# Gated layers of a four-layer trunk: each depthwise convolution in four pieces of four rounds in place of eight pieces of two

## The chip, the cores and the metric

The kernel runs on one core of a Trainium2 chip. The metric is the device time of one execution in microseconds. TensorE (PE in the profile) multiplies, its weight loads are shown apart as PEld; VectorE is DVE, ScalarE is ACT, GpSimd is POOL, and SyncE (SP) issues most of the DMA.

## What is computed

The input x has 512 channels of 64x64 pixels in float32. Four layers follow each other, each as x + f(groupnorm(x)): layer 0 is attention with eight heads, layers 1 and 2 are gated convolutions, layer 3 is a linear attention. The change touches layers 1 and 2, whose f is this (cut to the core; `conv1x1` is a matrix product over channels with a bias):

```python
fused = conv1x1(x, w_in, b_in)              # 512 -> 1024 channels
pwa = fused[:, :128]
abc = fused[:, 128:]                        # 896 channels, 7 groups of 128
dw0, dw1, dw2 = split(dwconv7(abc, dw_w, dw_b), (128, 256, 512))
h = pwa * dw0
h = conv1x1(h, pw0_w, pw0_b) * dw1
h = conv1x1(h, pw1_w, pw1_b) * dw2
x = x + conv1x1(h, w_out, b_out)
```

`dwconv7` is a depthwise 7x7 convolution: every channel with its own 49 taps.

## The kernel before

x stays in SBUF as X, four groups of 128 channels by 4096 pixels. `_attention` does layer 0, `_gated_convs` (lines 1110 to 1388) layers 1 and 2 in one loop over the layers, `_linear_attention` layer 3.

The depthwise convolution runs on TensorE. Each group of 128 channels is written to DRAM as planes (`_PlaneConv.put` and `take`, lines 938 to 977, tile `plane`, DRAM tensor `F`): the pixels of a channel are split by row modulo 4 and column modulo 8 into 32 planes. A convolution then is a product with small matrices T that carry taps from 32 planes to 32 planes. For one group `_PlaneConv.conv` (line 1014) works in `FORM.nr` = 16 rounds. A round is 24 products: 3 row offsets, 2 halves `rho`, 4 column groups `g`, each with a 64x32 tile of weights and 128 columns; each product is two weight loads and two matmuls in the trace, so a round has 48 matmul records. Four rounds fill a pair of PSUM banks (`ps_cv`, four banks, so two pairs), which VectorE transposes to the result `h` (line 1060); after the last round it transposes four quarters of `h` (line 1066), and ScalarE adds a bias to each (line 1317).

What a round reads is loaded by `load` (line 979) for two rounds at a time (NL = 2): SyncE issues one DMA for T and two for S, and ScalarE copies each 32 partitions of S, shifted, to 32 others (line 1006). Four buffers of each are there. `ahead` loads the first four rounds before a convolution begins; within it, round r loads what round r+4 needs.

`conv` is a generator. Between its pieces `convolve` (line 1311) puts other work in the program: parts of the input products of later groups (`group`, seven steps of a product scheme with seven instead of eight multiplications, lines 1230 to 1260), the products of the gates (`gate`, line 1262) and of the output (`output`, line 1277). They are 128x128 tiles by 512 columns, each two weight loads and two matmuls in the trace, into four banks `ps`, and leave by VectorE and by ScalarE's `kept` copies (line 1209). Where a piece ends is set here:

```python
for r0 in range(0, f.nr, f.rounds):
    ps = [self.psum.tile([P, BLK], FP, tag="mm", name="ps_cv") for _ in range(2)]
    for r in range(r0, r0 + f.rounds):
        if r % f.run == 0 and r > r0:
            yield
        if r % self.nl == 0:
            if r + f.rounds < f.nr:
                self.ready.append(self.load(i, hf, wT, r + f.rounds))
            w, S = self.ready.pop(0)
...
    if r0 + f.rounds < f.nr:
        yield
```

`f.rounds` is 4, and `f.run` is 2: a piece has two rounds, and each convolution eight pieces. `convolve` shares out the work in between: it has a list with a weight for each item, computes `parts = FORM.nr // FORM.run` (line 1324), and after each piece hands out items up to an equal share; the last quarter of the list is kept for the four quarters at the end.

TensorE's order is that of the program: `_PlaneConv.matmul` (line 933) pins each product to it, which is why all of them bear line 933 in the profile. The other engines' order is made by the layer that records the program[...].

Layer 3 uses `_PlaneConv` too, with `FORM3`, whose rounds have 16 products and whose pieces have four rounds; the change doesn't touch it.

## Time and profile before

| | us |
|---|---|
| median of three runs | 3827.91 |
| lowest, highest | 3826.85, 3833.11 |
| span of the profiled execution | 3828.3 |
| first and last convolution matmul of layers 1 and 2 | 2330.7, 3133.7 |

In the stretch from 2320 to 3130 us:

| engine, operation | count | mean ns |
|---|---|---|
| PE matmul of a convolution, 64x32 tile, 128 columns | 10656 | 272 |
| PE matmul of w_out, 128x128 tile, 512 columns | 347 | 602 |
| ACT copy within S | 224 | 1269 |
| DVE transpose of ps_cv to h | 110 | 1048 |
| DVE transpose within h | 52 | 1227 |

A matmul's mean is from its start to its modelled end; matmuls overlap, so the distance from one start to the next is shorter than that, and a row of the timeline that merges many of them is read by the start of the row after it. The page divides the span into 40 slices of 95.7 us. "Issue" is time in which an engine waited for nothing that the profile shows.

### The profile page before, as it was taken

How to read it: one execution, taken by the hardware profiler on the slowest of the kernel's cores; microseconds unless marked ns; L12 is line 12 of the kernel's file. 1: busy time of each engine (PE TensorE's matmuls, PEld its weight loads, DVE VectorE, ACT ScalarE, POOL GpSimd, SP SyncE). 2: the span in 40 equal slices, each digit the busy share in tenths (PEclk: the TensorE clock that was granted, in tenths of full speed). 3: DMA queues.
4: the chain of work that ended last, by engine and by line, in shares of the span. 5: the costliest groups of instructions: out<-in, count | busy, mean ns of one | idle time of the engine just before them, and what ended most of it. 6: DMA issues, size and time to landing. Idle time of an engine off the chain costs nothing. (4 is left out here: it accounts for less than half of the span.)

```text
span 3828.3 us, 81625 instructions
## 1 busy us (share of the span) xinstructions
PE 3752.0 (98%) x35294; PEld 1657.9 (43%) x35294; DVE 2688.1 (70%) x3242; ACT 2069.3 (54%) x2998; POOL 132.2 (3%) x112
## 2 busy tenths in 40 slices
PE   6999999999999999999999999999999999999999
PEld 5633334333365333343333334554445544455543
DVE  6577787777765777876776757766677677665437
ACT  3577774777735777746665655663246632355210
POOL 0000000000000000000000000000000000122112
PEclk9999999999999999999999999999999999999999
DMA  2000000000000000000000015772057730564312
GB/s 100 9 1 1 1 1 9 1 1 1 1 1 9 1 1 1 1 9 1 1 1 1 1 49 168 198 201 81 13 157 194 199 102 27 151 178 103 97 56 91
DMA packets 178413, 212.91 MB, mean 56 GB/s; under 512 B 13032, under 2 KB 121832, under 8 KB 177920
## 3 DMA queue, kind: packets, MB, share of 16 engines
q1 hardware_dynamic: 151232, 148.46, 14.5%
q10 hardware_dynamic: 26784, 59.11, 4.2%
q8 instruction: 280, 4.59, 0.5%
q14 instruction: 85, 0.70, 0.1%
q0 software_dynamic: 32, 0.06, 0.0%
HBM read 147.81 MB, written 59.77 MB: 54 GB/s over the span
## 5 line engine op out<-in xcount | busy, mean ns | idle before, releaser
L753 ACT ACTIVATE pt<-ps_s,A 128x512 f32<-128x512 f32 x2048 | 1286.3, 687 | 534.8 <-PE ps_s L745 527.1
L832 DVE TENSOR_TENSOR acc<-acc,pt 128x1024 f32<-128x1024 f32 x960 | 1174.1, 1223 | 327.8 <-ACT pt L753 300.8
L745 PE MATMUL ps_s<-O,K 64*64 64x512 f32 x8192 | 1111.6, 589 | 0.0
L745 PEld LDWEIGHTS ps_s<-O,K 64*64 64x64 f32 x8192 | 334.3, 133 | 553.8 <-issue 307.1
L765 PE MATMUL av<-pt,O 64*64 64x512 f32 x4096 | 558.2, 590 | 0.9 <-ACT pt L753 0.9
L765 PE MATMUL av<-pt,V 64*64 64x512 f32 x4096 | 554.4, 590 | 0.0
L1006 ACT COPY S<-S 32x1295 f32<-32x1295 f32 (+1 forms) x272 | 341.4, 1256 | 217.4 <-DMA S<-F 105.6
L765 PEld LDWEIGHTS av<-pt,O 64*64 64x64 f32 x4096 | 171.5, 133 | 276.1 <-issue 254.9
L765 PEld LDWEIGHTS av<-pt,V 64*64 64x64 f32 x4096 | 168.3, 133 | 281.0 <-issue 270.3
L933 PE MATMUL ps<-diff,w_sum 128*128 128x512 f32 x516 | 242.0, 601 | 3.1 <-DVE w_sum L441 1.9
L933 PEld LDWEIGHTS ps_cv<-S,T 64*32 64x32 f32 x13824 | 194.1, 105 | 111.5 <-issue 73.0
L933 PE MATMUL ps_cv<-S,T 64*32 64x128 f32 x13824 | 233.6, 273 | 5.0 <-issue 2.4
L933 PE MATMUL ps<-h,w_out_L 128*128 128x512 f32 x512 | 229.6, 599 | 1.5 <-DVE X L1287 1.4
L454 DVE TENSOR_TENSOR diff<-X 128x512 f32<-128x512 f32 x200 | 134.0, 683 | 83.1 <-PE ps L933 46.4
L383 ACT ACTIVATE X<-X,gn_less 128x512 f32<-128x512 f32 x122 | 77.3, 709 | 152.0 <-DVE gn_less L125 152.0
L933 PE MATMUL ps<-X,w_in_L 128*128 128x512 f32 x304 | 145.8, 611 | 10.8 <-ACT w_in_L L391 5.4
L933 PE MATMUL ps<-h,pw_L 128*128 128x512 f32 x320 | 143.8, 599 | 1.9 <-DVE h L1275 1.6
L933 PEld LDWEIGHTS ps<-h,w_out_L 128*128 128x128 f32 x512 | 94.0, 190 | 118.3 <-issue 96.5
L933 PEld LDWEIGHTS ps<-diff,w_sum 128*128 128x128 f32 x516 | 94.6, 190 | 116.8 <-issue 106.5
L454 DVE TENSOR_TENSOR diff<-X,diff 128x512 f32<-128x512 f32 x200 | 135.3, 683 | 12.9 <-PE ps L933 11.3
L1060 DVE STREAM_TRANSPOSE h<-ps_cv 128x512 f32<-128x512 f32 x112 | 109.2, 1048 | 48.6 <-PE ps_cv L933 48.2
L933 PE MATMUL ps<-agg,w_proj 128*128 128x512 f32 x256 | 118.5, 602 | 1.0 <-DVE turned L1060 0.9
(233 smaller groups left out, 3324.7 us busy)
## 6 DMA issues: line engine op xcount, KB each, us to landing
T<-in_L_T_dram SPq DMA_DIRECT2D x112, 384.0 KB, 4.6
F<-plane ACTq DMA_DIRECT2D x112, 324.0 KB, 3.5
S<-F SPq DMA_DIRECT2D x224, 162.0 KB, 4.6
S<-G SPq DMA_DIRECT2D x96, 153.0 KB, 4.3
G<-plane ACTq DMA_DIRECT2D x48, 289.0 KB, 2.5
row<-G SPq DMA_DIRECT2D x48, 272.0 KB, 3.3
T<-in_L_T_dram SPq DMA_DIRECT2D x48, 256.0 KB, 4.1
out_dram<-y SPq DMA_DIRECT2D x32, 256.0 KB, 2.0
```

Of the source, the lines that this page charges most:

```text
L383: self.nc.scalar.activation(xs, xs, AF.Identity, bias=less)
L454: yield eng.tensor_tensor(t[j][c], a(c), b(c), ALU.subtract)
L745: nc.tensor.matmul(ps[ts(half, D), ts(h, BLK)], K[rows, t * P + half * D : t * P + (half + 1) * D], QO[pair][rows, cols], start=True, stop ...
L753: exp = nc.scalar.activation(pt[:, ts(h, BLK)], ps[:, ts(h, BLK)], AF.Exp, bias=A[:, t, h : h + 1])
L765: nc.tensor.matmul(av[half][rows, :], v[keys, t * P + h * D : t * P + (h + 1) * D], pt[keys, ts(h, BLK)], start=(t == 0), stop=(t == NT - 1),)
L832: add = nc.vector.tensor_add(acc, acc if u > 1 else first, pt)
L933: self.tc.keep_in_program_order(self.nc.tensor.matmul(*args, **kw))
L1006: nc.scalar.copy(second, first)
L1060: nc.vector.transpose(out, src)
```

## The change

One number of the form of layers 1 and 2 changes, `run` from 2 to 4:

```diff
-FORM = _Form(2, 1, 4, 8, 1, 2, 3, 1, (-1, -1, -1, -1), (0, 0, 0, 0, -1, -1, -1, -1))
+FORM = _Form(4, 1, 4, 8, 1, 2, 3, 1, (-1, -1, -1, -1), (0, 0, 0, 0, -1, -1, -1, -1))
```

The inner `yield` of `conv` is then never reached, so that a piece is the four rounds of one pair of banks, 192 matmul records, and a convolution has four pieces. `parts` in `convolve` becomes 4, so the same items are handed out in stretches of about twice the length. The number of products, loads, copies and transposes stays as it is. The loads of rounds r+4 and r+6 are issued in the program with no other work in between. `run` is used nowhere else; the data in DRAM, the buffers and the banks are as before.

## The prediction

> **What bounds the kernel now.** I read the page first: engines and slices, the groups of TensorE instructions by shape, the instruction queues under DMA. Then the timeline of TensorE inside the two gated layers, which the change alone touches (2331 to 3134 us of the span), and the waits there.

> ```profile
> span 3828.3 us, 81625 instructions
> PE 3752.0 (98%) x35294; PEld 1657.9 (43%) x35294; DVE 2688.1 (70%) x3242; ACT 2069.3 (54%) x2998; POOL 132.2 (3%) x112
> PEclk9999999999999999999999999999999999999999
> ...
> q8 instruction: 280, 4.59, 0.5%
> ```

> TensorE sets the end: 98% busy at full clock, VectorE and ScalarE have room. What shortens TensorE's own sequence shortens the kernel, and what makes it stand still lengthens it. The q8 line (transfers, MB, share of the DMA engines) is used below.

> ```profile
> 3050.28 1.59 PE L933 MATMUL ps_cv<-S,T 64*32 64x128 f32 x96
> 3051.80 2.84 PE L933 MATMUL ps<-h,w_out_L 128*128 128x512 f32 x6
> 3054.57 1.60 PE L933 MATMUL ps_cv<-S,T 64*32 64x128 f32 x96
> 3056.10 2.84 PE L933 MATMUL ps<-h,w_out_L 128*128 128x512 f32 x6
> ...
> 3411.03 2.20 PE L933 MATMUL ps_cv<-S,T 64*32 64x128 f32 x128
> 3413.16 5.42 PE L933 MATMUL ps<-agg,w_proj 128*128 128x512 f32 x12
> ```

> Pieces of convolution alternate with stretches of dense products; the next row's start says what a row really takes. A piece of two rounds is 96 matmul records; start to start it takes 1.525 us (1.53, 1.52 here). Dense stretches of 4, 6, 8, 10 and 12 records take 1.914, 2.773, 3.631, 4.489 and 5.348 us: 0.429 each and 0.198 once per stretch. Pieces of 128 records in the last layer take 1.961 to 1.978 at best, so a conv record costs (1.97-1.525)/32 = 0.0140, and 1.525-96x0.0141 = 0.17 us is paid once per piece.

> ```profile
> 2413.85 1.98 PE L933 MATMUL ps<-X,w_in_L 128*128 128x512 f32 x4
> 2415.77 1.54 PE L933 MATMUL ps_cv<-S,T 64*32 64x128 f32 x90
> 2417.66 0.42 PE L933 MATMUL ps_cv<-S,T 64*32 64x128 f32 x6 [0.35 <-issue]
> ```

> From the waits of the same stretch, 2320 to 3130 us:

> ```profile
> PEld ps_cv L933 <- issue: 55.1, 75, 1.0
> PEld ps_cv L933 <- ACT S L1006: 19.7, 26, 0.8
> ```

> Here a piece stops after 90 of its 96 matmuls, with nothing in the profile to wait for ("issue"). Six pieces of the 112 do this, with 0.25 to 0.88 us lost, 3.5 us in all. Counting TensorE's instructions (weight load and matmul each one), the six resume at 40299, 41323, 42603, 42859, 43627 and 55402: whole multiples of 256 apart, to one instruction. Queue q8 has 280 transfers of 16 KB for TensorE's some 71,200 instructions, one per 256, and the transfer in question began 2.45 to 2.77 us before each resume. These stops are instruction fetch.

> [...] 0.17 + 0.198 us per pair of changes between 64x32 and 128x128 tiles. [...] 192 instructions in 1.36 us (0.0071 each) beat the fetch.

> **The change, part by part.** The order of TensorE's instructions in the built program shows 56 pieces of 192 records in place of 112 of 96; matmuls are the same, and 12 semaphore waits are added among some 24,000 instructions (nothing).

> (1) Fewer changes of tile shape. 112-56 = 56 pairs go, each 0.17+0.198 = 0.366 us: -20.5 us, all on TensorE, so all on the path.

> (2) Instruction fetch. In the kernel before, a block of 256 instructions can never lie in one piece (192), so it always takes in a dense stretch of at least 8 instructions: the shortest blocks take 1.525+1.914+0.4 = 3.8 us (the trace's least are 3.73 to 3.84). The fetch of a block is asked for about when its predecessor is entered. From that entry to the transfer's start the trace has two clusters, 0.6 to 1.0 and 1.5 to 2.3 us, earlier or below zero where a dense stretch let the sequencer run ahead (by up to some 40 instructions); from the transfer's start to use 2.2 to 2.8. Sum 3.2 to 4.3 us against 3.8: it nearly always just fits, and six times doesn't. That fit is the cover, and the change removes it: a piece now has 384 instructions, and a block wholly inside takes 256x0.0071 = 1.81 us. The stop is then 3.2-1.81 = 1.4 to 4.3-1.81 = 2.5 us.
> How many: laying the 256-grid of the six stops over the changed order, 29 of 95 blocks in these layers lie wholly in one piece (the kernel before: none); by proportion it would be (384-256)/404 = 32%, 30 blocks. 15 of them begin 57 or more instructions into the piece, past the sequencer's lead: 15 x 1.95 = 29 us. 14 begin within the first 43, where the lead may have called the fetch during the dense stretch: between 0 and 2.2, I take 1.1: 15 us. Some four more take in a last dense instruction or two, 0.5 each: 2. Sum +46 us, bounds 27 (15x1.4 + 14x0.4) and 76 (29x2.5 + 4). The 3.5 us of today's six stops go.

> (3) ScalarE, SyncE, DMA. Loads (one T, two S each) stay eight per convolution; two now come at the head of a piece together, and a few w_out loads of SyncE move by one or two loads. Buffers (four) come free one piece earlier or later, so from free to use there are two double stretches and a piece (2x3.6+3.04 = 10.3 us) where there were four single stretches and three pieces (12.2). Landing takes 4.6 us (S) and two copies 2x1.27, 7.1: 3 us spare. The four S copies of a piece stand closer, so a `kept` copy (0.69) can stand behind one or two more; its waits on TensorE today are 10.3 us at weight loads, most of it hidden. I take 0, bounds 0 and +6; gain excluded, nothing here gets shorter.

> (4) VectorE, PSUM. Same eight transposes (1.05) and four (1.23) per convolution, in pairs after each piece. Longest burst: six w_out products in 5.3 us against two transposes and six 0.73 additions, 6.4; the first product ends at 0.9, its bank is free at 2.9, the fifth wants it at 3.4 (four banks). No stop: 0. Conversely five data waits behind today's pieces (at 2397, 2515, 2885, 2924 and 3002 us; 0.84 to 1.51 each, 5.3 in all) may vanish under fetch stops, as other engines catch up: 0 to -5, I take 0.

> Sum: 3828.3 - 20.5 - 3.5 + 46 = 3850.3. The profiled span (3828.3) and the median of the runs shown (3827.9) agree to 0.4, so 3850 us.

> **The rivals.** (A) is the forecast: slower, 3850; own range 3832 to 3880 by its bounds.
> (B) Faster: the fetch keeps up. Mechanism: the sequencer's lead over the array. If it asks for each block long before the predecessor is entered, blocks arrive in time, only (1) stays: 3828.3-20.5-3.5 = 3804. For it: transfers have begun 1 to 7 us before that entry where dense stretches stood ahead (they get longer now), and 14 of 29 blocks begin near one. Against: inside pieces transfers begin 0.6 us after entry at the earliest, and the six stops exist. It decides where the mean stop of the 29 falls under 24/29 = 0.83 us, i.e. entry to use under 2.64 us; the trace has 3.2 there at best.
> (C) Slower through data: the second pair of rounds in a piece, with no dense stretch ahead of it any more, waits for its S copy. With the longest such wait of today (0.8) in each of 56 pieces: +45-20.5-3.5 = 3849 without (A), about 3895 on top of it. For it: ScalarE stands 105.6 us waiting for S transfers in these layers. Against: the 3 us to spare in (3).
> (D) The change doing nothing it says is excluded by the built order (56 pieces); that (1) and (2) cancel within 0.2% (under 7.7 us) is the low end of (A): stops of 0.6 to 1.1 us a block.

> **How the numbers follow.** A 0.65, B 0.15, D 0.08, C (with A or alone) 0.12. A change of 0.2%, 7.7 us, is about what a measurement of this kernel can tell from no change. Faster is B, 0.15; same is D, 0.08; slower is A and C, 0.77. Range: up to A's upper bound, 3880, leaving some 0.07 of C out; down to 3812, between B and D, leaving most of B out (0.13).

> **What would show it.** Pieces of 192 records: undisturbed 2.88 us start to start; about half should be interrupted inside by one "issue" gap of 1 to 2.5 us, all on the 256-grid, some 2.5 us after a q8 transfer began. Issue gaps at conv weight loads grow by some 40 us; TensorE's busy share falls. Dense stretches keep 0.429 per record. If pieces run 2.88 us throughout, (2) is wrong and B holds; if gaps end with an S copy rather than "issue", C. The size of a stop, not the count, is the least sure term.

## The result and the profile after

The changed kernel takes 3861.36 us (median of 5 runs, 3860.07 to 3866.26); the kernel before, with its runs beside these, 3830.03 (5 runs, 3826.85 to 3833.50). The ratio is 1.0082, 95% interval 1.0071 to 1.0093: slower by 31 us where 22 were forecast. The profiled spans are 3859.8 and 3828.3, 31.5 apart.

From the page of the changed kernel:

```profile
span 3859.8 us, 81643 instructions
PE 3745.8 (97%) x35294; PEld 1667.7 (43%) x35294; DVE 2689.0 (70%) x3242; ACT 2066.5 (54%) x2998; POOL 131.6 (3%) x112
PEclk9999999999999999999999999999999999999999
...
q8 instruction: 280, 4.59, 0.5%
```

TensorE has as many instructions and less busy time (3745.8 for 3752.0), in a longer span: it stands still more. The timeline of TensorE in the gated layers shows where (columns: start, time taken, then the instructions; idle time ahead of them in brackets):

```profile
2908.63 0.65 PE L933 MATMUL ps_cv<-S,T 64*32 64x128 f32 x25 [2.37 <-issue]
...
2912.83 2.96 PE L933 MATMUL ps_cv<-S,T 64*32 64x128 f32 x192
2915.73 1.98 PE L933 MATMUL ps<-diff,w_sum 128*128 128x512 f32 x4
...
2510.57 2.63 PE L933 MATMUL ps_cv<-S,T 64*32 64x128 f32 x169
2515.82 0.64 PE L933 MATMUL ps_cv<-S,T 64*32 64x128 f32 x23 [2.62 <-issue]
2516.39 1.98 PE L933 MATMUL ps<-diff,w_sum 128*128 128x512 f32 x4
```

An undisturbed piece of 192 records runs from 2912.83 to 2915.73, 2.90 us (the least in the stretch is 2.84). The piece at 2510.57 stops after 169 records, waits 2.62 us for nothing that the profile shows, and ends at 2516.39. From the waits of the same stretch, 2320 to 3141 us (who waited for whom: us in all, times, longest):

```profile
PEld ps_cv L933 <- issue: 71.8, 68, 2.9
PE ps_cv L933 <- issue: 35.6, 28, 2.6
PEld ps L933 <- ACT kept L1209: 18.2, 10, 5.6
PE ps L933 <- ACT kept L1209: 10.4, 8, 4.8
PEld ps_cv L933 <- ACT S L1006: 6.1, 8, 0.8
```

The second, third and fourth of these rows in the kernel before:

```profile
PE ps_cv L933 <- issue: 2.2, 5, 0.7
PEld ps L933 <- ACT kept L1209: 10.3, 12, 1.7
PE ps L933 <- ACT kept L1209: 5.4, 7, 1.4
```

What grows most is the idle time without a cause in the profile, and more ahead of the convolution's matmuls (2.2 to 35.6 us) than of their weight loads (55.1 to 71.8).

From the starts of TensorE's records I took, for each, what the distance to the next exceeds the usual one by, and sorted the excess between the first and the last convolution matmul of layers 1 and 2. A stop is put down to the fetch if it ends where a block of 256 instructions begins, on the grid that the kernel before gave; dense matmuls at twice their usual distance are counted apart.

| excess, us (cases) | before | after | difference |
|---|---|---|---|
| stops where a block of 256 begins | 3.7 (8) | 44.3 (33) | +40.6 |
| dense matmuls at half rate, 0.853 in place of 0.429 | 2.0 (5) | 7.8 (18) | +5.8 |
| all other waits of TensorE | 15.9 | 19.9 | +3.9 |
| changes of tile shape saved, 56 x 0.366 | | | -20.5 |

The sum is +29.8 against 31.5 between the spans; 1.7 us stay unexplained. The last row isn't measured: it is the price of the prediction.

That the stops on the grid are stops of the fetch has two signs. In both kernels every stop of over 0.2 us between two matmuls of a piece lies on the grid, 6 of 6 before and 30 of 30 after, and none elsewhere. And those of the changed kernel end 2.2 to 2.9 us after a transfer of q8, the queue that carries the instructions, began; that queue made 280 transfers of 16 KB for some 71,200 instructions of TensorE, one to some 256.

The half rate follows some of the long stops, and a long data wait too. Windows of the changed kernel (from and to in us, length, busy time and records of TensorE, granted clock, DMA share, GB/s), around a stop of 2.18 us in the piece from 2420 and after a data wait at 2927:

```profile
2418.00:2424.00 6.00, 4.96 (x194) 1.00 0.45 145
2426.00:2429.00 3.00, 3.00 (x5) 0.52 1.03 276
...
2921.00:2926.00 5.00, 5.00 (x198) 1.00 0.77 245
2931.00:2937.00 6.00, 4.56 (x6) 0.52 0.02 4
```

The granted clock is 1.00 before and 0.52 after: five or six dense matmuls take twice their time. By the clock record of the trace half the clock is granted for 23.9 us of these layers (3.4 in the kernel before): 10.2 after three of the stops, which end at 2412.03, 2424.94 and 2624.13 us, 6.8 after the data wait, and 6.8 at the change from layer 1 to layer 2, where the kernel before has its 3.4. The page's 40 slices are too coarse to show it.

The length of a stop doesn't decide: the three longest, of 2.6 to 2.9 us, end at 2450.68, 2515.82 and 2908.63 and are followed by the full clock. In the clock record the five stretches at half clock begin whole multiples of 3.41 us apart (4, 62, 103 and 152 after the first) and last one or two such steps. In the step ahead of its half clock TensorE stood for 1.93, 1.99 and 2.25 us at the three stops. Each of the three longest is cut by a border between steps, with 1.93, 1.64 and 1.26 us of idle time at most in one step. So at these six stops it was the idle time within a step that went with the clock of the next: 1.99 and 2.25 us with half, 1.64 and less with the full clock, 1.93 once with each. A rule is not shown by this. The second step at half clock after the data wait follows one with 1.17 us of idle time, and in layer 3 the same record has half the clock from 3439.85 to 3443.26 after a step in which TensorE was busy throughout:

```profile
3436.44:3439.85 3.41, 3.41 (x26) 1.00 1.01 301
3439.85:3443.26 3.41, 3.41 (x60) 0.50 0.71 147
```

### The profile page after: what moved, and what is told of

The parts are those of the page before. It is cut to its first block, busy times and chain, and to the rows that moved or that the text cites. A ratio compares the mean times of both kernels' runs of the same rounds, so it can differ in the third digit from the quotient of the medians.

```text
span 3859.8 us, 81643 instructions
## 1 busy us (share of the span) xinstructions
PE 3745.8 (97%) x35294; PEld 1667.7 (43%) x35294; DVE 2689.0 (70%) x3242; ACT 2066.5 (54%) x2998; POOL 131.6 (3%) x112
## 3 DMA queue, kind: packets, MB, share of 16 engines
q8 instruction: 280, 4.59, 0.5%
## 5 line engine op out<-in xcount | busy, mean ns | idle before, releaser
L1006 ACT COPY S<-S 32x1295 f32<-32x1295 f32 (+1 forms) x272 | 341.4, 1256 | 235.9 <-DMA S<-F 117.7
L933 PE MATMUL ps_cv<-S,T 64*32 64x128 f32 x13824 | 228.1, 272 | 39.4 <-issue 35.6
L933 PEld LDWEIGHTS ps_cv<-S,T 64*32 64x32 f32 x13824 | 197.2, 105 | 108.0 <-issue 89.7
L933 PE MATMUL ps<-diff,w_sum 128*128 128x512 f32 x516 | 242.2, 602 | 1.4 <-DVE plane L973 1.4
L933 PE MATMUL ps<-h,w_out_L 128*128 128x512 f32 x512 | 225.3, 596 | 0.5 <-DVE X L1287 0.5
L933 PE MATMUL ps<-X,w_in_L 128*128 128x512 f32 x304 | 150.4, 627 | 17.0 <-ACT kept L1209 10.4
L933 PEld LDWEIGHTS ps<-diff,w_sum 128*128 128x128 f32 x516 | 97.9, 193 | 123.1 <-issue 113.3
L933 PEld LDWEIGHTS ps<-h,w_out_L 128*128 128x128 f32 x512 | 95.4, 190 | 119.0 <-issue 101.6
L933 PE MATMUL ps<-h,pw_L 128*128 128x512 f32 x320 | 143.5, 601 | 0.5
L933 PE MATMUL ps<-agg,w_proj 128*128 128x512 f32 x256 | 117.7, 599 | 0.0
```

The source lines that it names most:

```text
L933: self.tc.keep_in_program_order(self.nc.tensor.matmul(*args, **kw))
L1006: nc.scalar.copy(second, first)
```

## The experiments

Theory: instruction fetch, block by block, as in step (2). Rivals: loads (a piece waits for its second pair of rounds), and long pieces as such. Ten kernels were run, in three groups, each with the kernel before beside it (its medians there: 3832.3, 3829.7 and 3832.4). A stop's place is counted in TensorE instructions from the first convolution matmul, modulo 256: 28 or 29 for all six stops of the kernel before and for all 30 inside pieces of the changed one.

**Shifting the grid.** In the changed kernel, ahead of the gated layers:

```diff
+    pad = bank_gn()
+    for _ in range(32):
+        pc.matmul(pad[0:32, 0:1], gmask[0:64, 0:32], gmask[0:64, 0:1], start=True, stop=True)
```

> The changed kernel (four pieces of four rounds) with 32 small extra matmuls (64x32 tiles, one column; 128 TensorE instructions) ahead of the gated layers, in a stretch where TensorE waits for the group norm anyway. They move every later instruction by half a block of 256. Fetch theory: the stops inside pieces keep their place on the 256-grid of instruction numbers, so counted from the first convolution matmul they move from 29 (modulo 256) to 157: other pieces and other points in them. 31 blocks lie wholly in one piece in place of 29, so about as many stops (some 33) and about the same sum (42 to 48 us); time 3855 to 3868, like the changed kernel's 3861. Loads theory (a piece waits for its second pair of rounds): the stops stay in the same pieces at the same points counted from the first convolution matmul, since no data moves; time 3861.

Measured: 3869.7 us, ratio to before 1.0099 (1.0084 to 1.0115). 29 stops inside pieces, 44.8 us, and every one of them at 156 or 157, none at 29. A piece of it, stopped with 63 records to go:

```profile
2502.67 1.14 PE L933 MATMUL ps_cv<-S,T 64*32 64x128 f32 x63 [2.65 <-issue]
2503.74 1.98 PE L933 MATMUL ps<-diff,w_in_L 128*128 128x512 f32 x4
```

The stops follow the instruction number and leave the places where data would be waited for. The time lies 2 us over the expected range; 3.5 us of it come ahead of the first convolution (2334.2 for 2330.7), so the extra matmuls weren't quite free.

**Taking the loads away.** Changed kernel; in the second run the kernel before:

```diff
-                    if r + f.rounds < f.nr:
-                        self.ready.append(self.load(i, hf, wT, r + f.rounds))
-                    w, S = self.ready.pop(0)
+                    if self.shared:
+                        if r + f.rounds < f.nr:
+                            self.ready.append(self.load(i, hf, wT, r + f.rounds))
+                        w, S = self.ready.pop(0)
+                    else:
+                        w, S = self.ready[r // self.nl % 2]
...
+        if not self.shared:
+            self.ready.clear()
```

> The changed kernel with the loads of T and S and ScalarE's copies within S left out for all but the first four rounds of each convolution; the later rounds use those again (so the convolutions compute something else; the products are as many and as large). Fetch theory: the stops remain, about 31 blocks lie wholly in one piece; with DMA nearly quiet a fetch may land somewhat sooner, so 30 to 45 us of stops, and a few us of ordinary data waits go: 3838 to 3858. Loads theory: without loads there is nothing to wait for, stops go, and with them some data waits: 3830 less 20 less 5 = 3800 to 3812.

> The kernel before (eight pieces of two rounds) with the loads and copies of T and S left out for all but the first four rounds of each convolution (later rounds use those again, so the convolutions compute something else). It is the base for the other kernels without loads. Fetch theory: the few fetch stops of the kernel before (3.5 us) shrink to 0 to 3, ordinary data waits hardly move: 3822 to 3829, so that four pieces without loads (measured 3832.9) are slower by 20.5 saved against some 26 us of stops: +4 to +10. Loads theory: without loads four pieces must be faster by the 20 us of saved changes, so this kernel would take about 3853.

Measured: four pieces without loads 3832.9 (1.0002, 0.9994 to 1.0011), eight pieces without loads 3820.9 (0.9974, 0.9962 to 0.9985). Without loads four pieces are still slower than eight, by 12.0 us of medians and 9.8 of spans (the two are of different groups). Four pieces are 5 us under their expected range, with 28.1 us of stops where 30 to 45 were expected; eight pieces are 1 us under theirs. TensorE's waits in the long pieces without loads:

```profile
PE ps_cv L933 <- issue: 22.0, 18, 1.8
PE ps L933 <- ACT kept L1214: 5.6, 7, 1.7
PE gn_ps L124 <- DVE gn_mv L95: 2.0, 1, 2.0
```

22 stops on the grid, 28.1 us (19 inside pieces, 25.8); in eight pieces one, 0.24. With -20.5 and +1.5 of other waits and 0.9 less at half rate the traces' sum is some +8. The loads theory, which wanted four pieces some 20 us faster, falls. But of the 31 us that the change costs with loads only some 10 to 12 are left: with loads and copies the stops are more and longer, 33 and 44.3 us. The transfers of q8 aren't what takes longer: from the start of one to the end of the stop it is 2.3 to 3.0 us without loads and 2.2 to 2.9 with them. So with loads it is the start of the fetch that comes later (the stops at blocks beginning late in a piece are 1.76 us on average with loads, 1.42 without); why stays open.

**Shorter pieces.** The kernel before with `run` 1:

```diff
-FORM = _Form(2, 1, 4, 8, 1, 2, 3, 1, (-1, -1, -1, -1), (0, 0, 0, 0, -1, -1, -1, -1))
+FORM = _Form(1, 1, 4, 8, 1, 2, 3, 1, (-1, -1, -1, -1), (0, 0, 0, 0, -1, -1, -1, -1))
```

> Pieces of one round; the work in between runs out of items in places, so the built order has 174 pieces in place of 112. Price of a change of tile shape and back 0.366 us: 62 x 0.366 = +22.7 us, fetch stops (3.5 us before) fall to 1 or 2: 3830 + 22.7 - 2 = 3851, range 3845 to 3857. If changing between the tile shapes were free at the device, and long pieces as such were the cost, shorter pieces would be no slower than the kernel before: 3825 to 3831.

Measured: 3863.3 (1.0079, 1.0062 to 1.0096), 31 us slower, 6 over the range. Fetch stops are 4.0 us, other waits 21.6 (5.7 more than before), half rate 3.8. Its timeline (a piece of 96 records, then one of 48):

```profile
2397.04 1.65 PE L933 MATMUL ps_cv<-S,T 64*32 64x128 f32 x96
2398.61 1.98 PE L933 MATMUL ps<-X,w_in_L 128*128 128x512 f32 x4
2400.53 0.94 PE L933 MATMUL ps_cv<-S,T 64*32 64x128 f32 x48
2401.39 1.98 PE L933 MATMUL ps<-diff,w_sum 128*128 128x512 f32 x4
```

A piece of 48 takes 0.868 us at the median, 48x0.0141 + 0.19. So the price per change is there, 0.19+0.198 = 0.39 us, some 24 us for 62; most of the rest of the 31 are ordinary waits, which I had left out. That changes are free, as the rival wanted, is excluded.

**Pieces of 256 instructions.** The kernel before, cut by row offsets in place of rounds (a round has three), with `parts` following:

```diff
+FORM.cuts = (8, 16, 24, 32, 40)
...
+                    at = r * f.by * f.bx + b + 1
+                    if f.cuts and at in f.cuts and at % (f.rounds * f.by * f.bx):
+                        yield
...
-            parts = FORM.nr // FORM.run
+            parts = len(FORM.cuts) + 1
```

> Pieces of eight row offsets (two and two thirds rounds, 256 TensorE instructions), six per convolution in place of eight; adjacent ones counted, 84 pieces for 112. Fetch theory: a block of 256 lies wholly in a piece only if it begins exactly with it, so stops stay as in the kernel before (2 to 5 us), while 28 changes of tile shape and back are saved, 28 x 0.366 = 10.2 us: 3830 - 10 = 3820, range 3815 to 3825. If the loss of the changed kernel comes from long pieces as such (loads bunched, other engines served late), pieces a third longer lose a third of it, about +10: 3840.

Measured: 3841.7 (1.0022, 1.0013 to 1.0032): 9 us slower than before, not 10 faster. The fetch part is nearly as expected: stops 7.8 us where 2 to 5 were expected, seven inside pieces. What I hadn't expected is ordinary waits, 26.7 us for 15.9. In the waits of 2320 to 3150 us:

```profile
PEld ps L935 <- ACT kept L1215: 24.8, 17, 3.4
PE ps L935 <- ACT kept L1215: 14.2, 13, 2.5
```

The same two rows are 10.3 and 5.4 us in the kernel before (shown above). So longer pieces have a second cost, which the rival of long pieces has right. Whether it is due to the loads the next run tells: six pieces with the edit that leaves the loads out, and five, for a dose between six and four (`FORM.cuts = (10, 20, 30, 40)`).

> Six pieces of eight row offsets, loads left out as in the base without loads. If what six pieces lost were data waits that the bunched loads cause, they go here, and the 28 saved changes show: 10 us under the base without loads, about 3815 (3812 to 3820). If longer pieces cost other engines something that has nothing to do with loads (copies out of PSUM served late), it stays about 5 to 10 us over the base.

> Five pieces of ten row offsets (320 TensorE instructions, the last of eight), 70 pieces, loads left out as in the base without loads. A dose between six and four pieces: 14 blocks of 256 lie wholly in one piece (six pieces 0, four pieces 31, of which 19 stopped at 1.36 us each without loads). Fetch theory: 14 x 19/31 x 1.36 = 12 us of stops against 42 x 0.366 = 15.4 saved: 3 us under the base without loads, about 3822 (3815 to 3830), with some 9 stops inside pieces. If stops grew with the piece's length alone and not with the blocks in it, six pieces would stop half as often as these.

Measured: six 3812.3 (0.9952, 0.9939 to 0.9966), five 3818.3 (0.9970, 0.9959 to 0.9981), in one group with eight pieces without loads, 3820.9. Six pieces save 8.6 us of the 10.2, their stops are 0.55 us, and kept waits are 7.3 and 3.3. Five pieces save 2.6 for the 3 expected; ten stops make 13.5 us, as one at 2471.93 does after 159 records:

```profile
2471.93 2.45 PE L935 MATMUL ps_cv<-S,T 64*32 64x128 f32 x159
2475.88 0.29 PE L935 MATMUL ps_cv<-S,T 64*32 64x128 f32 x1 [1.49 <-issue]
2476.10 1.98 PE L935 MATMUL ps<-diff,w_sum 128*128 128x512 f32 x4
```

So without loads the price list holds, to within some 5 us, over eight, six, five and four pieces (0, -8.6, -2.6, +12): saved changes against blocks that lie in one piece, of which there are 0, 0, 14 and 31. It jumps between six and five, where a piece first exceeds 256 instructions. So the second cost of six pieces comes from what these runs left out: the loads, or ScalarE's copies within S that follow them.

**Freeing ScalarE of the copies.** Six pieces with loads, the second of the two copies within S on GpSimd; then both copies; then the second one in the kernel before:

```diff
             if rho and self.shared:
                 nc.vector.tensor_copy(second, first)
+            elif not self.shared and rho:
+                nc.gpsimd.tensor_copy(second, first)
             else:
                 nc.scalar.copy(second, first)
```

> Six pieces of eight row offsets with all loads, but the second of the two copies within S that follow each load goes from ScalarE to GpSimd, which is idle in these layers. If six pieces with loads lost their saving (measured +8 in place of -10 against the kernel before) because ScalarE's copies of PSUM stand behind copies within S that wait for their DMA, half of that loss goes: TensorE's waits for kept copies (24.8 us at weight loads in six pieces, 10.3 in the kernel before) fall, time 3816 to 3828. A GpSimd copy is put at 2.6 to 3.5 us from its 1.0 to 1.4 us for 512 elements; at one per 8 us it keeps up. If the lost time has another cause, or GpSimd disturbs VectorE: 3838 or more.

> As the kernel with the second copy on GpSimd, but both copies within S go there. ScalarE then never waits for these loads: kept waits fall to those without loads (7.3 us at weight loads) and time to 3812 to 3820, if GpSimd keeps up. Two copies of 2.6 to 3.5 us per load are 5 to 7 us, with a load every 6 to 8 us of the stretch: if it doesn't keep up, pieces wait for S and the time is over 3840.

> The kernel before (eight pieces of two rounds) with the second copy within S on GpSimd: the control for the same move in six pieces. Its data waits for kept copies are small (10.3 us at weight loads, most of it hidden), so 3822 to 3830; if six pieces gain only by this move, both gain the same, and six pieces stay 8 us over eight.

Measured: 3849.1 (1.0043, 1.0029 to 1.0057), 3866.8 (1.0094, 1.0078 to 1.0109) and 3847.4 (1.0036, 1.0023 to 1.0050): all slower than with ScalarE, and all three misses. GpSimd keeps up but for 2.5 us of matmul waits when it has both copies; a copy takes 1.36 to 1.39 us, half of what I had put. But TensorE's waits for kept copies don't fall (23.7 us at weight loads with one copy moved, 35.7 with both), and some of VectorE's work slows down. With both moved, groups of 2320 to 3150 us:

```profile
L1008 POOL COPY S<-S 32x1295 f32<-32x1295 f32 x221 | 307.0, 1389 | 587.0 <-DMA S<-F 560.1 <-PE ps_cv L935 15.4 <-PE ps L935 3.8
L456 DVE TENSOR_TENSOR diff<-X 128x512 f32<-128x512 f32 x101 | 82.8, 836 | 38.3 <-PE ps L935 38.1
```

The same VectorE subtraction takes 681 ns in six pieces without the move; additions with one operand in PSUM stay at 682 ns. In the kernel before the move takes the kept waits at weight loads from 10.3 to 23.9 us, so it has a cost of its own and is no clean test. Against that control six pieces are only 1.7 us behind, where they were 9 behind without the move. So my reading that kept copies are late because copies within S stand ahead of them on ScalarE is neither shown nor excluded; why loads delay kept copies more in longer pieces stays open. No version that does all the work beat the kernel before.

## Why the prediction was right, step by step

**(1)** The changes of tile shape: right in sign and about in size. Pieces of 192 records take 2.84 to 2.90 undisturbed, where 2.88 was said. The price is known only between two measures. Two undisturbed pieces of 96 take 2x1.525 = 3.05 us and one of 192 at least 2.84, so 0.21 goes, and with 0.198 for the dense stretch 0.41 per pair. Six against eight pieces without loads save 8.6 us for 28 pairs, 0.31 each. The 0.366 of the prediction lies between; for 56 pairs that is 17 to 23 us. What the runs price is going from convolution to dense products and back; that the cause is the tile shape, and nothing else that changes there, was my reading and was not shown.

**(2)** The fetch: the mechanism was right, and so was the sum, +40.6 us for 46-3.5 = 42.5, in part by luck. That 33 stops stand against 29 blocks and some four more is luck: 17 and 6 of them belong to the 29 blocks, 10 to blocks with some dense instructions.

By place: 17 of the 29 blocks begin over 45 instructions into their piece, and all 17 stop, 1.76 us on average (15 blocks at 1.95 were said). 12 begin within the first 45 and lose 0.50 on average, half of them nothing (14 at 1.1 were said). The line at 45 is drawn after the traces; the prediction had its own between 43 and 57, and a block right at it lost 2.9 us, which stands with the 17. The other runs bear the line out: in the shifted kernel all 21 blocks of the first kind stop, at 1.71, without loads all 18, at 1.42, and in five pieces without loads all 8. Of the second kind none loses more than 0.3 in the two runs without loads (13 and 6 blocks), but in the shifted kernel five of eight stop, by up to 2.9 us.

So the lead of the sequencer, an estimate of some 40 instructions (in the traces before and after, transfers of q8 begin up to 44 and 40 of them ahead of the entry of their block's predecessor), covers a block without loads and about every second one with them. In the changed kernel it saved some 9 us more than I had given it. Stops at blocks that take in some dense instructions were more than I had put, about 8 us for 2. These two errors largely cancel. From the entry of a block to the use of the next the stops give 1.81+1.76 = 3.6 on average (3.0 to 4.7 at the ends), near the middle of the 3.2 to 4.3 taken, with wider ends.

**(3), (4)** Other engines: 0 with bounds of -5 and +6; other waits rose by 3.9, within them. The largest single one is in the rows of `kept` above: at 2927 TensorE stands 4.8 us for a kept copy while ScalarE copies within S and waits for their DMA, which is what step (3) named and priced at nothing. Six pieces show that ordinary waits can grow by more (+10.8).

**What was missing** is the half clock, +5.8 us, after three of the stops and after the data wait. It and the data waits, 3.9, less the 1.9 by which the fetch stayed under its sum, make 7.8 of the 9.5 us between the 22 forecast and the 31.5 of the spans. Rival (B) set its own mark, a mean stop of the 29 blocks under 0.83 us; it was 1.24 (17 at 1.76 and 12 at 0.50). (C) did not happen: no stop inside a piece ends with a copy of S, and the weight loads of the convolution wait less for S than before (6.1 us for 19.7). The data waits that grew stand at dense products, for `kept` copies.

## What to carry to other kernels

## What was not expected of the hardware

- In the changed kernel's gated layers half the clock was granted in steps of 3.41 us, 23.9 us in all. A stop of 2.2 us within one step was followed by a step at half clock, with five dense matmuls at twice their time (granted 0.52); three stops of 2.6 to 2.9 us across a border were followed by the full clock.
- With the loads and the copies within S the fetch stops are more and longer: 33 and 44.3 us with them, 22 and 28.1 without, with the blocks inside pieces about the same (29 and 31).
- GpSimd copied a 32x1295 float32 tile in 1.36 to 1.39 us, near ScalarE's 1.27, but with both copies moved there VectorE's 128x512 subtraction from SBUF went from 681 to 836 ns, and its additions from PSUM stayed at 682.
